# Image chunks in the later passes of a Fourier-layer kernel: one 1 MB load on SyncE and one 1 MB store on GpSimd, in place of two half transfers each on SyncE

## The chip, the cores and the metric

The kernel runs on one core of a Trainium2 chip. The metric is the time of one execution on the device, in microseconds (us). Five engines run their own instruction streams in order: TensorE (PE), VectorE (DVE), ScalarE (ACT), GpSimd (POOL) and SyncE (SP). Any of the last three may issue DMA transfers between the chip's memory (HBM) and the on-chip buffers; here SyncE issues nearly all of them.

## The reference

The input is 64 images of 256 x 256 and 64 text blocks of 77 x 256. A tokenizer of four Fourier layers runs over the images with 32 channels; its result, with the text rows below it, goes through one attention layer and a feed-forward layer that treats half of the rows. Cut to what matters here:

```python
def _fourier_layer(v, W1, W2):            # v: [64 images, 32 channels, 256, 256]
    x_ft = jnp.fft.rfft2(v)
    out1 = jnp.einsum('bixy,ioxy->boxy', x_ft[:, :, :M1, :M2], W1)     # M1 = M2 = 12
    out2 = jnp.einsum('bixy,ioxy->boxy', x_ft[:, :, -M1:, :M2], W2)
    ...
    return jnp.fft.irfft2(out_ft, s=(Sx, Sy))
...
for i in range(L):                        # L = 4
    x1 = _fourier_layer(v, W1, W2)
    x2 = jnp.einsum('bcxy,cd->bdxy', v, w_w[i]) + w_b[i][None, :, None, None]
    v = x1 + x2
    mean = jnp.mean(v, axis=(0, 2, 3), keepdims=True)
    var = jnp.var(v, axis=(0, 2, 3), keepdims=True)
    v = (v - mean) * jax.lax.rsqrt(var + BN_EPS)
    v = v * bn_g[i][None, :, None, None] + bn_b[i][None, :, None, None]
    if i < L - 1:
        v = jax.nn.relu(v)
out = jnp.einsum('bcxy,cu->bxyu', v, q_w) + q_b
```

The normalization is over all 64 images, so every layer has to be complete before its successor can be scaled. The whole of v is 64 x 32 x 256 x 256 numbers of fp32, 537 MB, and is kept in HBM between layers.

## The kernel before, in words

The work is four stages, one after the other. Between them lies `mix` (L428), which multiplies the few kept Fourier coefficients of all images by the layer's weights, writes the result to HBM (`mix_d`) and derives the normalization.

- **Pass 0** (`layer` with i = 0) builds the first v from the coefficients and the image itself and stores it. It loads no v.
- **Passes 1 and 2** (`layer` with i = 1 and 2), the *later passes*, load v of the pass before, compute the new v and store it. `src` and `dst` are two sets of 64 HBM tensors [128, 8, 8, 256] that change roles.
- **The last stage** loads v once more (L980, rows of 8 KB) and does the fourth layer, attention and feed-forward for each image.

An image is cut into eight chunks t = 0 to 7 of 128 partitions x 8 rows x 256 numbers, 1 MB each. In HBM a chunk is 8 KB in a row for each partition. The steps of `layer` for a chunk t of image b are:

- `ld` (L652) loads the chunk into a `vin` tile, in two halves of 512 KB, with rows of 4 KB. The pool `li` has four such tiles in the later passes.
- `pre` (L676) is PE's work: the inverse transform (L682) and the product of the loaded chunk with the layer's weights (L693), both into two pairs of PSUM banks. It then takes a `vo` tile; the pool `lo` has four.
- `evA` and `evB` (L701) evict one bank pair each, with the maximum against zero, into a half of `vo`. The letter `a` or `d` in the order says whether ACT (L705) or DVE (L707) does it.
- `st` (L711) stores `vo` to `dst`, in two halves.
- `turn` (L716) transposes `vo` on DVE (L719) for the next forward transform.
- `prod` (L724) multiplies `vo` with the next layer's weights on PE (L730), and `sqA`/`sqB` (L736) sum its squares on ACT (L741). These give the next variance.

For an image, `am` (L643) has SyncE load the mixed coefficients into one of two `ams` tiles (`load_am`, L621) and POOL scale them (`scale_am`, L628, at L631). `sp` (L662) uses these on PE and `spT` transposes them into the `y_` tiles that `pre` reads. The steps `y` (L752), `half`, `zt`, `x` (L786) and `xo` do the forward transform of the finished image, and `xs` (L803) stores its 72 KB of coefficients.

PSUM is a ring of four slots of two banks, taken by `take` and given back by `close`. `pre` and `prod` take two slots each.

The order of all this is written out by hand. `ORDER[1]` (L137) is one round of the later passes. `@1` marks a step of the next image, `@2` of the one after, `@-1` of the last. Each engine gets its own instructions in just this order. SyncE's share of a round is

```
ld2@1 st4 st5 ld0@1 ld7 ld3@1 st6 ld1@1 st2@1 ld5@1 st0@1 am@2 st7 st1@1 ld4@1 ld6@1 xs@-2 st3@1
```

and POOL's is `am@2` alone. A step that has to wait holds up all that follows it on its engine. PE's `pre` steps come as 5, 6, 2@1, 0@1, 3@1, 7, 1@1, 4@1, so a `vo` tile goes to the fourth chunk after in this list.

Of the kernel before, what the change touches and what calls it, by code (L numbers as in the profile page):

```python
# [153 lines left out]
def tile_fno_fusion_transformer(ctx: ExitStack, tc: tile.TileContext, a, cst_d, grid_d, out):  # L154
    nc = tc.nc
# [390 lines left out]
    def layer(i, st, src, dst, acc):  # L546
# [7 lines left out]
        with ExitStack() as cx:  # L554
# [64 lines left out]
            y_, t32, vin, vo, half_, zts = {}, {}, {}, {}, {}, {}  # L619
# [31 lines left out]

            def ld(b, t, e):  # L652
                vin[b, t] = ip.tile([128, 8, S], F32, name="vin")
                for n in range(2):
                    rows = slice(4 * n, 4 * n + 4)
                    nc.sync.dma_start(vin[b, t][:, rows], src[b][:, t, rows])

            def sp(b, h, e):
                ps = take(("sp", b, h), 1)[0]
# [49 lines left out]
                return run  # L709

            def st_(b, t, e):  # L711
                for n in range(2):
                    rows = slice(4 * n, 4 * n + 4)
                    nc.sync.dma_start(dst[b][:, t, rows], vo[b, t][:, rows])
# [87 lines left out]
            def xs(b, n, e):  # L802
                nc.sync.dma_start(xh_d[i][:, b, :], xos.pop(b).rearrange("p g k -> p (g k)"))  # L803

            run = dict(
                am=am, lx=lx, ld=ld, sp=sp, spT=spT, pre=pre, evA=ev(0), evB=ev(1), st=st_, turn=turn,
                prod=prod, sqA=sq(0), sqB=sq(1), y=y, half=half, zt0=zt(0), zt1=zt(1), x=x_, xo=xo, xs=xs,
            )
# [53 lines left out]
    src = vd[L % 2]  # L862
# [87 lines left out]
    rows = [128, 128, TXT]  # L950
# [283 lines left out]
```

## Time and profile before

| | |
|---|---|
| median of three runs | 11274.17 us (11272.87 to 11285.87) |
| the profiled execution | 11293.58 us, its span 11291.7 us |
| PE, DVE, ACT, POOL busy in the span | 94%, 75%, 57%, 13% |
| HBM read and written | 1733.60 MB and 1696.92 MB |
| v<-vo stores issued by SyncE | 3072 of 512 KB, 1024 in each pass |
| vin<-v loads issued by SyncE | 2048 of 512 KB, 1024 in each later pass |
| PE clock granted, mean | 0.983 |

The profile shows one execution, with times from the start of its span. A group of instructions is named by line, engine, operation and tiles (`v<-vo` writes the HBM tensors v from tile vo). A wait is put down to what came last before the waiting instruction could start. `SPq` is SyncE's instruction stream with its DMA issues; `PEld` is PE's loading of weights, which runs beside its matmuls. Busy shares of PE come from modelled ends of matmuls, so a busy PE is not a PE at its peak. The DMA share is the mean busy share of 16 DMA engines.

### The profile page before, as it was taken

Reading aid. Unit: us, or ns where it says so; the run is one execution under the profiler, and the core shown is the slowest. Engines: PE = TensorE matmul, PEld = TensorE weight load, DVE = VectorE, ACT = ScalarE, POOL = GpSimd, SP = SyncE. Lnnn points to the kernel's source line nnn. Section 1 sums busy time; section 2 is a strip of 40 time slices with the busy share of each in tenths; the row PEclk is TensorE's granted clock in tenths of the full one; section 3 lists DMA queues with packets and bytes.
Section 4 is the critical chain, followed back from the end, with each engine's and each line's share of the span. In section 5 each row is a group of like instructions: output and inputs, shape, how many; then the busy total and the mean of one; then the engine's idle time right before and its main releaser. Section 6 shows DMA issues by size and latency. Waiting matters only on the chain.

```text
span 11291.7 us, 409300 instructions
## 1 busy us (share of the span) xinstructions
PE 10625.0 (94%) x182550; PEld 5738.0 (51%) x182550; DVE 8446.5 (75%) x10381; ACT 6473.1 (57%) x10673; POOL 1442.4 (13%) x2179
## 2 busy tenths in 40 slices
PE   6999999998999999999799999999996999999999
PEld 3555555554444444444444444444443666666666
DVE  6888888887777777777677777777775666666665
ACT  5777777775566655566555566655563333333333
POOL 1111111110000000000000000000000333333333
PEclk8999999998999999999899999999998999999999
DMA  6776676678999999999899999999998555555553
GB/s 213 247 250 244 249 247 248 246 253 320 383 376 382 380 377 372 374 379 379 305 375 380 380 376 378 381 380 376 372 379 291 226 227 228 227 227 228 226 227 140
DMA packets 972544, 3457.29 MB, mean 306 GB/s; under 512 B 149784, under 2 KB 199320, under 8 KB 903832
## 3 DMA queue, kind: packets, MB, share of 16 engines
q1 hardware_dynamic: 905344, 3366.80, 77.8%
q0 software_dynamic: 58288, 60.60, 2.3%
q8 instruction: 1428, 23.40, 0.8%
q10 hardware_dynamic: 7144, 3.72, 0.1%
q14 instruction: 340, 2.79, 0.1%
HBM read 1733.60 MB, written 1696.92 MB: 304 GB/s over the span
## 4 chain that ended last, share of the span: by engine, by line
PE 62%; DMA 20%; DVE 9%; ACT 3%; issue 3%; SPq 2%; POOL 0%; ACTq 0%; DVEq 0%; POOLq 0%
PE ring L752 15%; DMA v<-vo 11%; PE ring L682 9%; PE ring L730 8%; DMA vin<-v 6%; PE ring L693 5%; PE hp L982 4%; PE ring L662 3%; PE pp L1145 3%; PE pp L1156 3%; PE ring L786 2%; DVE vo L707 2%; PE pp L1110 2%; PE pp L1175 2%; PE pp L1072 1%
## 5 line engine op out<-in xcount | busy, mean ns | idle before, releaser
L741 ACT ACTIVATE ring<-ring 128x1024 f32<-128x1024 f32 x3072 | 3115.8, 1014 | 1188.4 <-PE ring L730 1119.5
L719 DVE STREAM_TRANSPOSE t<-vo 128x2048 f32<-128x2048 f32 x1536 | 3465.7, 2286 | 20.9 <-DVE vo L707 0.9
L730 PE MATMUL ring<-vo,w 32*32 32x512 f32 x49152 | 2413.1, 600 | 85.0 <-ACT vo L705 68.3
L707 DVE TENSOR_SCALAR vo<-ring 128x1024 f32<-128x1024 f32 x1280 | 1544.5, 1221 | 1199.7 <-PE ring L693 806.6
L705 ACT ACTIVATE vo<-ring 128x1024 f32<-128x1024 f32 x1792 | 1791.7, 1023 | 1044.1 <-PE ring L693 500.9
L752 PE MATMUL ring<-t,cst 32*32 32x512 f32 x49152 | 2072.0, 599 | 51.0 <-issue 44.9
L752 PEld LDWEIGHTS ring<-t,cst 32*32 32x32 f32 x49152 | 913.4, 103 | 925.6 <-issue 622.6
L730 PEld LDWEIGHTS ring<-vo,w 32*32 32x32 f32 x49152 | 803.2, 103 | 1070.2 <-issue 407.1
L693 PE MATMUL ring<-vin,ws 32*32 32x512 f32 x32768 | 1287.8, 603 | 22.9 <-issue 16.2
L682 PE MATMUL ring<-cst,y 24*128 24x256 f32 x16384 | 1230.3, 402 | 77.0 <-DVE vo L707 61.7
L682 PEld LDWEIGHTS ring<-cst,y 24*128 24x128 f32 x16384 | 789.5, 185 | 993.2 <-DVE vo L707 392.4
L631 POOL TENSOR_TENSOR ams<-ams,bns 48x512 f32<-48x512 f32 x384 | 400.5, 1043 | 6989.4 <-DMA ams<-mix 6510.1
L670 DVE STREAM_TRANSPOSE y<-ring 128x1024 f32<-128x1024 f32 x384 | 763.1, 1987 | 329.5 <-PE ring L662 328.5
L682 PE MATMUL ring<-mv,y 29*128 29x256 f32 x8192 | 705.3, 403 | 36.3 <-ACT ring L741 19.6
L682 PEld LDWEIGHTS ring<-mv,y 29*128 29x128 f32 x8192 | 456.9, 185 | 369.0 <-ACT ring L741 209.3
L786 PEld LDWEIGHTS ring<-cst,zt 128*128 128x128 f32 x4608 | 533.6, 193 | 177.1 <-ACT vo L705 114.2
L762 ACT COPY half<-ring 128x1024 f32<-128x1024 f32 x192 | 194.4, 1013 | 731.4 <-PE ring L752 731.4
L1183 POOL DMA_DIRECT2D out_dram<-o x1024 | 508.2, 505 | 659.0 <-DVE o L1178 616.9
L741 ACT ACTIVATION_READ_ACCUMULATOR ring<-ring 128x1 f32 x3072 | 585.6, 191 | 0.0
L786 PE MATMUL ring<-cst,zt 128*128 128x96 f32 x4608 | 565.6, 280 | 6.1 <-DVE zt L770 5.7
L770 DVE STREAM_TRANSPOSE zt<-ring 128x1024 f32<-128x1024 f32 x192 | 377.4, 1965 | 248.1 <-PE ring L752 248.1
L662 PE MATMUL ring<-ams,cst 49*128 49x512 f32 (+1 forms) x1536 | 450.6, 642 | 99.1 <-POOL ams L631 37.2
(374 smaller groups left out, 9762.6 us busy)
## 6 DMA issues: line engine op xcount, KB each, us to landing
v<-vo SPq DMA_DIRECT2D x3072, 512.0 KB, 7.8
vin<-v SPq DMA_DIRECT2D x2048, 512.0 KB, 9.1
ch<-v SPq DMA_DIRECT2D x512, 1024.0 KB, 12.5
mix<-ob SPq DMA_DIRECT2D x96, 512.0 KB, 5.6
ams<-mix SPq DMA_DIRECT2D x384, 96.0 KB, 8.0
xin<-in_x_dram SPq DMA_DIRECT2D x16, 1024.0 KB, 6.5
mv<-in_x_dram POOLq DMA_DIRECT2D x256, 64.0 KB, 7.4
out_dram<-o POOLq DMA_DIRECT2D x1024, 16.0 KB, 3.0
```

Of the source, the lines that this page charges most:

```text
L662: nc.tensor.matmul(ps[:, n, :], lhsT=EX[hv, 128 * h:128 * h + 128], rhs=ams[b % 2][hv], start=True, stop=True, skip_group_check=True,)
L670: nc.vector.transpose(y_[b, h].rearrange("p q c -> p c q"), ring[key][0][1].rearrange("p n (c k) -> p (n c) k", k=32),)
L682: nc.tensor.matmul(ps[n][:, 256 * r:256 * r + 256], lhsT=y_[b, t // 4][32 * n:32 * n + K, q:q + 4, :].rearrange("p q c -> p (q c)"), rhs=m ...
L693: nc.tensor.matmul(ps[n][32 * j:32 * j + 32], lhsT=ws[32 * n:32 * n + 32], rhs=v[32 * n:32 * n + 32, 2 * j:2 * j + 2, :], start=False, sto ...
L705: nc.scalar.activation(to, ring[key][h][1], AF.Relu)
L707: nc.vector.tensor_scalar(to, ring[key][h][1], 0.0, None, ALU.max)
L719: nc.vector.transpose(t32[b, t // 2][:, :, 8 * (t % 2):8 * (t % 2) + 8, :].rearrange("p y s c -> p s y c"), vo[b, t].rearrange("p s (y l) ...
L730: nc.tensor.matmul(ps[n][32 * j:32 * j + 32], lhsT=w4[i + 1][32 * n:32 * n + 32], rhs=vo[b, t][32 * n:32 * n + 32, 2 * j:2 * j + 2, :], st ...
L741: nc.scalar.activation(ps, ps, AF.Square, accum_out=acc[:, at:at + 1])
L752: nc.tensor.matmul(ps[n][32 * j:32 * j + 32], lhsT=FYT[32 * n:32 * n + 32, k, :], rhs=t32[b, j][32 * n:32 * n + 32, k].rearrange("p s c -> ...
L786: nc.tensor.matmul(ps[:, 0, 96 * g:96 * g + 96], lhsT=zt_[:, h, k0:k0 + 4, :].rearrange("p k c -> p (k c)"), rhs=FX[:, h, 48 * r:48 * r + ...
L1183: nc.gpsimd.dma_start(out[b, 64 * n + 16 * g:64 * n + 16 * g + 16].rearrange("(p t) d -> p t d", t=2), o[32 * g + 8 * n:32 * g + 8 * n + 8 ...
```

## The change

In `ld` the two half loads become one load of the whole chunk, still issued by SyncE. In `st` the later passes issue one store of the whole chunk from GpSimd's queue; pass 0 keeps its two half stores on SyncE. The order, the pools and all other steps are as they were. SyncE's share of a round of the later passes is then the `ld` steps, the loads of `am` and `xs`; POOL's is `st4 st5 st6 st2@1 st0@1 am@2 st7 st1@1 st3@1`.

```diff
             def ld(b, t, e):
                 vin[b, t] = ip.tile([128, 8, S], F32, name="vin")
-                for n in range(2):
-                    rows = slice(4 * n, 4 * n + 4)
-                    nc.sync.dma_start(vin[b, t][:, rows], src[b][:, t, rows])
+                nc.sync.dma_start(vin[b, t], src[b][:, t])
...
             def st_(b, t, e):
+                if i:
+                    nc.gpsimd.dma_start(dst[b][:, t], vo[b, t])
+                    return
                 for n in range(2):
                     rows = slice(4 * n, 4 * n + 4)
                     nc.sync.dma_start(dst[b][:, t, rows], vo[b, t][:, rows])
```

## The prediction, made before the changed kernel had run

> **What bounds the kernel now.** I read the page's slices first, because the change touches only two of the four stages. One core runs the work; the bandwidth row shows where.
>
> ```profile
> DMA  6776676678999999999899999999998555555553
> GB/s 213 247 250 244 249 247 248 246 253 320 383 376 382 380 377 372 374 379 379 305 375 380 380 376 378 381 380 376 372 379 291 226 227 228 227 227 228 226 227 140
> ```
>
> A slice is 282 us. Slices 10 to 19 and 20 to 30, near 377 GB/s, are the two later passes (i=1, 2), which load and store every chunk; the first pass only stores, the last stage only loads. Next the engines in one of these passes, from the windows view (columns: window, its length, busy time of PE, PE's weight loads, DVE, ACT, POOL, clock, DMA share, GB/s).
>
> ```profile
> 2700.00:5400.00 2700.00, 2588.29 (x55106) 1224.46 (x55105) 2021.65 (x1128) 1625.06 (x2559) 123.24 (x118) 1.00 0.98 377
> ```
>
> PE and DMA both look full; neither quite is. An image takes 45.3 us (SyncE's ams loads start at 3626.7, 3671.5, 3717.3, 3762.4, 3808.2, 3853.2). PE's steps, at the closest spacing that the timeline shows (32 small matmuls in 1.07 us, 16 of L682 in 1.08, the 24 of L786 in 2.84, L662 in 1.06), add to about 8x1.07x3 + 8x1.08 + 2.84 + 2.1 = 39 us. An image moves 16.8 MB of chunks and 0.27 MB of the rest. In 1 us slices of one image the DMA runs flat at about 415 GB/s for some 25 us and swings between 25 and 430 in the other 20, with a mean near 330; 17.05 MB at 415 would be 41 us. So both have about a tenth to spare, and dependencies between them make up the 45.3 us. The chain of waits of that window gives DMA v<-vo 20.1% and DMA vin<-v 11.7% of it. Who waited says what this costs (engine, line, releaser: total us, times, longest):
>
> ```profile
> ACT vo L705 <- DMA v<-vo: 125.6, 94, 3.1
> DVE vo L707 <- DMA v<-vo: 124.4, 95, 3.0
> PEld ring L662 <- POOL ams L631: 37.4, 33, 1.3
> PEld ring L693 <- DMA vin<-v: 12.0, 24, 1.0
> ```
>
> The evictions of a new chunk wait until the store of the chunk that held the same vo buffer (four of them) has landed; the two engines wait side by side, so it is one loss of about 125 us in 2700. Why stores land late shows in the view of L714, in the later pass and then in the first:
>
> ```profile
> DMA to landing us min/median/max: 2.8/8.9/12.7
> DMA to landing us min/median/max: 2.6/4.9/10.0
> ```
>
> The same 512 KB takes 8.9 us instead of 4.9, since it stands behind loads in one queue. It is also issued late: SyncE's own waits in that pass are
>
> ```profile
> SPq L714 <- ACT vo L705: 495.3, 127, 8.2
> SPq L714 <- DMA v<-vo: 312.0, 347, 2.3
> SPq L714 <- DMA vin<-v: 240.8, 273, 2.4
> ```
>
> that is, it stands at a store until ACT has evicted, with loads behind it, and then is held back by its full DMA queue, one issue each 1.5 us.
>
> **What the Trainium skill says.** "DMA: Bandwidth & Descriptors", section "Issuing engines are not separate DMA queues": transfers of all issuers run on the same 16 DMA engines and interleave, so another issuer brings no bandwidth. I count none; no run shown here puts two large streams on two queues. The same page, "Queues, rings and completion order": each DMA engine takes turns between the queue rows that hold work, a packet at a time. A store on its own row then passes the loads' backlog. The trace shows the one-queue side of it only (8.9 against 4.9 us). "SBUF — State Buffer", section "SBUF: two separate sides": GpSimd cannot write its descriptors while VectorE holds both ports in a two-port mode. "VectorE: DVE Perf Modes", "Why PSUM operands drop a tier": fp32 from PSUM runs at the base rate. The trace agrees: L707 reads PSUM, 1024 elements in 1221 ns, and the transpose L719 2048 in 2286 ns, both over 1 ns an element. I expect no such lock.
>
> **The change, part by part.** An image now costs SyncE 16 half loads, 16 half stores, two ams loads and one xh store; after it, 8+2+1. There are 128 images in the two passes.
>
> *Halves to wholes.* 4 KB rows become 8 KB rows. In the last stage 1 MB loads with 8 KB rows (ch<-v) run near 419 GB/s when the queue is full (9030 to 9045 us), against 415 with 4 KB rows: 1%. DMA volume is not what ends the image, so I cost this at nothing; if it were, 1% of 41 us is 0.4 us an image, 52 us. Against it, a whole chunk lands as one, so the first half's eviction can wait up to 0.5 MB/415 GB/s = 1.3 us longer where it waits at all. That is 1.6 places an image (95 in 59.6), 265 us at worst; the earlier issue of the store covers it.
>
> *Stores to GpSimd.* 8 issues an image. The nearest rows are POOL's loads of mv (L638) and xh (L845), 563 and 552 ns each, the latter for 4 MB: 4.5 us on an engine with 2.1 us of work in 45.3, hidden. A lower bound is zero, since POOL is off the path. The descriptors cost latency too: 64 KB loads from GpSimd take 7.4 us to land in pass one beside 4.9 us for 96 KB from SyncE, so I add 2.5 us. Half of 415 GB/s moves 1 MB in 5.1 us, with 2.5 us more 7.6; alone at full rate 5.0. Before: 8.9 from issue, and issued 2 to 13 us after the evictions (st6: evictions end near 3611.7, issue 3614.0; st3 of the next image: 3626.7 and 3639.6). The tightest reuse I find is chunk 2 to chunk 1 of an image, 3618.4 to 3630.7, 12.3 us: 7.6 fits.
>
> *Loads alone on SyncE.* They go when vin is free: chunk 4 at about 3627 instead of 3635.3, chunk 0 at 3607.2 instead of 3609.2. Little is gained directly, since PE waits for vin 12.0 us in the pass, most of it the 0.33 us that a weight load idles anyway. ams is asked for at about 3621 instead of 3626.7.
>
> *Sum.* Windows 2700 to 5400 and 5700 to 8400 hold 119 of the 128 images (factor 1.074). Store waits: DVE 124.4+133.6 = 258, times 1.074 = **277 us**. What passes to PE is a choice: in the image read, chunk 3's evictions wait 1.03 us and PE's next step, prod, shows a 0.77 us gap, but other waits fall where PE has work or waits for a PSUM pair anyway. I take half, **139**. ams: 37.4+33.3 = 71 us of weight-load idle in 63 waits, 1.1 each, where 0.9 is usual before that step: 0.25 us x 63 x 1.074 = **17**. vin: 25.3 us, 0.33 of each usual: **10**. Together 166, of an upper bound of 277+76+27 = 380. The profiled execution took 11293.6 us (span 11291.7), 19.4 above the median of 11274.2. 11293.6 - 166 = 11127.6, or **11108** on the median's scale. After the store waits, what is late next is the eviction-to-PSUM-ring step (DVE vo <- PE ring L693 and the weight loads held by DVE vo).
>
> **Rivals.**
>
> *All of it passes through.* The chain's 32% of DMA speaks for it; PE's 39 us and DMA's 41 leave room. 380 us: 10894. Chance 0.13.
>
> *Nothing passes through.* In the first pass stores hardly stall (DVE 5.1 us, ACT 24.3 in 1800), yet an image takes 36.4 us where the same PE count gives 30.6: nearly 6 us of gaps from evictions and PSUM alone, as many as here. Then a freed store only lets another wait surface: 0 to 30 us gained, 11244 to 11274. Against: DVE is busy 89% there and 75% here. Chance 0.13.
>
> *Slower: stores behind the ams wait on GpSimd.* POOL runs in order. Its list is now st4, st5, st6, st2, st0, am (wait for the ams load, then two scalings, 2.2 us), st7, st1, st3. Today ams takes 10 us to land and POOL waits for it in nearly every image. Asked for at 3621 it lands at 3631, is scaled by 3633, and three stores leave by 3634.5; 3 MB at half rate is 15.2 us, plus 2.5: 3652. Chunk 3's buffer is wanted by chunk 5's evictions at 3652.5. It just fits; if ams lands later than 11 us after its issue, or if the loads get more than half the DMA, every us is lost. With ams as late as today the store is 5 us late; half passed on is 2.5 x 128 = 320, less the 166: 11430. For it: a margin under 1 us. Against: loads end before that, so stores get more than half, and ams stands behind fewer loads. Chance 0.17.
>
> *The change does not do what it says*, 8 KB rows being cut to 4 KB packets: in the last stage 59,296 packets are of 8 KB or more, about 464 loads x 128 rows, so rows travel whole. It would cost nothing in any case.
>
> **How the numbers follow.** Forecast 0.57, all 0.13, nothing 0.13, slower 0.17. Within 0.2%, 22 us (about what a measurement of this kernel can tell from no change), lies some 0.08 of the third case; its rest gains just over that. Faster 0.75, same 0.08, slower 0.17. The range reaches down to 10960, which leaves out the farthest part of the full gain (some 0.06), and up to 11340, which takes in the milder half of the slower case.
>
> **What would show it.** Right: the waits of ACT and DVE on v<-vo fall below a third, the image falls to 44 us (GB/s of the slices up to 388), SyncE no longer waits for ACT, POOL shows 1024 issues near 0.55 us, DMA leaves the chain. Wrong: evictions wait as much as before with stores landing over 12 us; POOL's st7 starts only after ams and evictions wait right after; or the store waits vanish and PE's gaps behind DVE and ACT grow by as much.

## The result and the profile after

The changed kernel takes **11313.56 us** (median, 11308.88 to 11326.04), the kernel before in the same runs 11274.56 (11265.47 to 11291.58). The ratio is 1.0034, 95% interval [1.0025, 1.0043]: 39 us slower, where 166 faster had been forecast. The profiled execution took 11314.35 us, 20.8 more than that of before; the two profiles thus show about half of the difference in the medians.

What the change was aimed at did move. The waits of the middle of pass 1 (2700 to 5400 us; total us, times, longest), then the chain of the whole span by engine, before and after:

```profile
DVE vo L705 <- PE ring L691: 353.0, 284, 4.2
PEld ring L753 <- issue: 257.0, 487, 2.9
DVE vo L705 <- DMA v<-vo: 107.8, 73, 3.9
ACT vo L703 <- DMA v<-vo: 71.9, 74, 3.2
PEld ring L691 <- DMA vin<-v: 1.3, 4, 0.3
```

```profile
PE 62%; DMA 20%; DVE 9%; ACT 3%; issue 3%; SPq 2%; POOL 0%; ACTq 0%; DVEq 0%; POOLq 0%
PE 73%; DVE 10%; DMA 9%; issue 4%; ACT 3%; SPq 0%; POOL 0%; ACTq 0%; DVEq 0%; POOLq 0%
```

With pass 2's window (ACT 61.0, DVE 36.8; before 131.8 and 133.6), the waits of evictions for stores fell from 257 us to 133 on ACT and from 258 to 145 on DVE: to half, not to nothing. PE's waits for vin are nearly gone, those for POOL's ams wholly. DMA fell from 20% to 9% of the chain and PE rose from 62% to 73%. Yet the window holds no more work (length, then busy time of PE, weight loads, DVE, ACT, POOL, clock, DMA share, GB/s):

```profile
2700.00:5400.00 2700.00, 2581.68 (x54896) 1220.74 (x54888) 2021.36 (x1126) 1621.09 (x2548) 374.41 (x592) 1.00 0.95 376
```

That is 54,896 matmuls in place of 55,106. Two landing views bear on why only half of the waits went: stores of L711, then loads of L654.

```profile
DMA to landing us min/median/max: 5.7/11.1/15.9
DMA to landing us min/median/max: 4.9/11.3/14.3
```

A 1 MB store lands 11.1 us after its issue; the forecast had 7.6. Its working took a single store with half of the bandwidth, but stores overlap. In this window the 114 of 474 that had no other store under way when they were issued landed in 8.3 us (median), those with one or two in 11.0 and 12.0. POOL's timeline shows three in a row after the scaling of ams:

```profile
3638.52 2.16 POOL L631 TENSOR_TENSOR ams<-ams,bns 48x512 f32<-48x512 f32 x2 [9.62 <-PE ring L660]
3640.63 1.64 POOL L711 DMA_DIRECT2D v<-vo  x3
```

They landed at 3648.7, 3651.2 and 3653.6.

**Where the gain went.** From the starts of PE's instructions in the trace I cut each round of the later passes in three (means over 103 rounds): the *store part*, from `pre` of chunk 3 to the first `sp`, where most late stores are waited for; the *y section*, from that `sp` to `pre` of chunk 4 (both `sp`, eight `y`, one `prod`); and the rest.

| us a round | store part | y section | rest | round |
|---|---|---|---|---|
| before | 10.43 | 13.48 | 21.53 | 45.44 |
| after | 9.74 | 14.23 | 21.67 | 45.64 |
| difference | -0.70 | +0.75 | +0.14 | +0.20 |

The store part gives back 0.70 us and the y section takes 0.75. The standard error of a mean is 0.05 us for the store part and 0.06 to 0.11 for the others. The net 0.20 x 128 is 25 us, near the 21 between the profiled executions. What PE lacks in the y section shows in the page's groups: L752 before and L753 after, the same matmuls and their weight loads (busy, mean ns | idle before, what ended most of it):

```profile
L752 PE MATMUL ring<-t,cst 32*32 32x512 f32 x49152 | 2072.0, 599 | 51.0 <-issue 44.9
L752 PEld LDWEIGHTS ring<-t,cst 32*32 32x32 f32 x49152 | 913.4, 103 | 925.6 <-issue 622.6
```

```profile
L753 PE MATMUL ring<-t,cst 32*32 32x512 f32 x49152 | 2116.8, 600 | 82.0 <-issue 75.4
L753 PEld LDWEIGHTS ring<-t,cst 32*32 32x32 f32 x49152 | 914.9, 103 | 998.5 <-issue 691.8
```

One matmul takes as long as before. What grew is "issue", time in which PE waited for nothing that the profile shows: 31 us before the matmuls, 69 before the weight loads. One line of the page's list of queues, which the prediction did not use, names a suspect (packets, MB, share of 16 engines):

```profile
q8 instruction: 1429, 23.41, 0.8%
```

PE runs 182,550 matmuls and as many weight loads. Spread over these 365,100 instructions, 23.41 MB is 64 bytes for each, and a packet of 16.4 KB is 256 of them. I take it from this count that the queue carries PE's own program, 7.2 packets in a round; if one comes late, PE stands still. The gaps fit: compared with the median gap at the same place of the round, PE loses over 500 ns 1.37 times a round before (1.40 us) and 1.98 times after (2.08 us). I call these gaps *stalls*. Some 63% of them, before, and 65%, after, end 1.25 to 1.5 us after the end of such a packet, where 5% of places picked at random lie. They also come back every 255.7 of PE's records, so they shift by a fixed step from round to round, as blocks of 256 instructions do.

The y section has most of the growth: its stalls went from 0.60 to 1.20 us a round, 0.60 of the 0.75 that it lost. Of those 58 stalls before and 118 after (112 rounds each), 57 and 108 end 1.2 to 1.6 us after a packet. PE's waits for the other engines did not grow there: its weight loads wait 1.7 us a round behind ACT, DVE and POOL before and 1.0 after. So in the kernel after, most of what the y section lost is PE without instructions.

### The profile page after: what moved, and what is told of

Same layout as the page of the kernel before. It is cut to its first block, busy times and chain, and to the rows that moved or that the text cites. A ratio compares the mean times of both kernels' runs of the same rounds, so it can differ in the third digit from the quotient of the medians.

```text
span 11312.5 us, 405471 instructions
## 1 busy us (share of the span) xinstructions
PE 10623.1 (94%) x182550; PEld 5739.4 (51%) x182550; DVE 8455.8 (75%) x10381; ACT 6479.4 (57%) x10673; POOL 1985.2 (18%) x3203
## 3 DMA queue, kind: packets, MB, share of 16 engines
q8 instruction: 1429, 23.41, 0.8%
## 4 chain that ended last, share of the span: by engine, by line
PE 73%; DVE 10%; DMA 9%; issue 4%; ACT 3%; SPq 0%; POOL 0%; ACTq 0%; DVEq 0%; POOLq 0%
PE ring L753 17%; PE ring L680 12%; PE ring L731 11%; PE ring L691 8%; DMA v<-vo 7%; PE hp L983 4%; DVE vo L705 4%; PE ring L787 3%; PE ring L660 3%; PE pp L1146 3%; PE pp L1157 3%; PE pp L1111 2%; PE pp L1176 2%; PE pp L1073 1%; DVE t L720 1%
## 5 line engine op out<-in xcount | busy, mean ns | idle before, releaser
L731 PE MATMUL ring<-vo,w 32*32 32x512 f32 x49152 | 2448.5, 600 | 53.1 <-ACT vo L703 32.6
L753 PE MATMUL ring<-t,cst 32*32 32x512 f32 x49152 | 2116.8, 600 | 82.0 <-issue 75.4
L753 PEld LDWEIGHTS ring<-t,cst 32*32 32x32 f32 x49152 | 914.9, 103 | 998.5 <-issue 691.8
L691 PE MATMUL ring<-vin,ws 32*32 32x512 f32 x32768 | 1241.6, 604 | 15.5 <-issue 15.0
L711 POOL DMA_DIRECT2D v<-vo x1024 | 549.9, 539 | 3727.7 <-DVE vo L705 2566.2
L787 PEld LDWEIGHTS ring<-cst,zt 128*128 128x128 f32 x4608 | 533.2, 193 | 175.3 <-ACT vo L703 110.5
L787 PE MATMUL ring<-cst,zt 128*128 128x96 f32 x4608 | 565.2, 279 | 7.4 <-DVE zt L771 7.2
```

Source lines behind the costliest of these rows:

```text
L691: nc.tensor.matmul(ps[n][32 * j:32 * j + 32], lhsT=ws[32 * n:32 * n + 32], rhs=v[32 * n:32 * n + 32, 2 * j:2 * j + 2, :], start=False, sto ...
L711: nc.gpsimd.dma_start(dst[b][:, t], vo[b, t])
L731: nc.tensor.matmul(ps[n][32 * j:32 * j + 32], lhsT=w4[i + 1][32 * n:32 * n + 32], rhs=vo[b, t][32 * n:32 * n + 32, 2 * j:2 * j + 2, :], st ...
L753: nc.tensor.matmul(ps[n][32 * j:32 * j + 32], lhsT=FYT[32 * n:32 * n + 32, k, :], rhs=t32[b, j][32 * n:32 * n + 32, k].rearrange("p s c -> ...
L787: nc.tensor.matmul(ps[:, 0, 96 * g:96 * g + 96], lhsT=zt_[:, h, k0:k0 + 4, :].rearrange("p k c -> p (k c)"), rhs=FX[:, h, 48 * r:48 * r + ...
```

## The experiments

Theory **F** (fetch): the transfers delay PE's instruction packets, most with two queues of 8 KB rows together, and PE stalls where its instructions are densest. Against it: **P**, stores held back behind the ams wait in GpSimd's order (the slower rival of the prediction); **G**, given back: evictions freed of stores wait for PSUM instead, so that no store wait is worth anything. Ratios are to the kernel before on the same chip.

**Whole chunks, one queue (e1).** To the kernel after:

```diff
-                    nc.gpsimd.dma_start(dst[b][:, t], vo[b, t])
+                    nc.sync.dma_start(dst[b][:, t], vo[b, t])
```

> Whole chunks both ways, but the stores stay on SyncE: the row size alone is changed, not the issuer. Three theories stand. Instructions: in the changed kernel PE's irregular stalls (over 500 ns beyond the usual gap at the same place of the round, most of them ending 1.25 to 1.5 us after an instruction packet has arrived) grew from 1.4 to 2.1 us a round, because two data queues of 8 KB packets stand before the instruction fetch; that ate what the freed stores gave. Given back: PE's gaps come from evictions and PSUM, and a store that lands earlier is worth nothing. POOL order: the stores behind the ams wait cost the time. Instructions theory: if the second queue does it, stalls stay at 1.4 us and the time is 11250 to 11280; if the 8 KB packets do it, stalls near 2 us and 11310 to 11360. Given back: 11275 within 15. POOL order: 11275 within 15, since GpSimd has no stores here.

11291.43 us, 1.001 [1.0001, 1.0018]. Round 45.40, y section 13.67.

**Halves, two queues (e2).** To the kernel before:

```diff
-                    nc.sync.dma_start(dst[b][:, t, rows], vo[b, t][:, rows])
+                    (nc.gpsimd if i else nc.sync).dma_start(dst[b][:, t, rows], vo[b, t][:, rows])
```

> Stores of the later passes on GpSimd, but all transfers stay halves with 4 KB rows: the issuer alone is changed. Instructions theory: if the second queue does it, stalls of 2 us a round and about 11310; if the packet size does it, stalls of 1.4 us, store waits halved and about 11200. Given back: 11275 within 15. POOL order: about 11310, as in the changed kernel, since the ams wait stands in GpSimd's list as there.

11277.11 us, 0.9996 [0.9988, 1.0005]. Store part 9.74 as in the kernel after, y section 13.70. So the second queue alone brings the gain of the store part. Most of it is given back: the y section takes 0.2 us of it and the rest of the round 0.24, where DVE now waits for stores 0.96 us a round (0.05 before). The time ends at nothing that can be measured. Neither the rows alone nor the queue alone lengthens the y section by more than about 0.2 us.

**After, with 4 KB rows (e5).** The HBM tensors become [128, 2, 8, 4, 256], so that a whole chunk has two rows of 4 KB a partition.

```diff
-    vd = [dram.tile([128, 8, 8, S], F32, name=f"v{b}_{n}") for n in range(2) for b in range(B)]
+    vd = [dram.tile([128, 2, 8, 4, S], F32, name=f"v{b}_{n}") for n in range(2) for b in range(B)]
...
-                    nc.gpsimd.dma_start(dst[b][:, t], vo[b, t])
+                    nc.gpsimd.dma_start(dst[b][:, :, t], vo[b, t].rearrange("p (h r) y -> p h r y", h=2))
```

> The changed kernel (one whole transfer of 1 MB each way, two queues), but v lies in HBM as two half chunks, so that every row is of 4 KB. So far: irregular PE stalls of over 500 ns are 1.4 us a round before, 1.6 and 1.3 with one queue of 8 KB rows, 1.4 and 1.5 with two queues of 4 KB rows, 2.0 and 2.1 with two queues of 8 KB rows. Instructions theory: an instruction packet waits for one packet of each data queue, so with 4 KB packets the stalls fall to 1.5 us and the time to that of the two queues of halves, 11260 to 11285. Whole-landing theory (a buffer that is released and filled as a whole is what costs, not the packet): stalls stay at 2 us or the time stays at 11313 within 10. Given back: 11275 to 11313, says little.

11349.78 us, 1.0064 [1.0051, 1.0077], and read by stage: y section 13.67, round 45.45, as in the kernel before. Nearly the whole loss is in the last stage, whose loads now have 4 KB rows as well: from the last matmul of the passes (L786, here L787) to the end of the span it takes 2778 us in place of 2717. With e1 and e2 this closes the square: only two queues **and** 8 KB rows together give the long y section.

It also shows that a short y section is not enough. The store part takes 9.66 us, 0.77 less than before, and yet the round is no shorter: the rest of the round grew by 0.56 us, with 1.75 us a round of DVE's waits for stores (0.05 before) and 0.83 us of stalls (0.53 before). Stalls come to 1.69 us a round in all, between before and after and over the 1.5 that F had. In e2 and in e5 the gain of the store part is thus lost without the long y section, in the rest of the round.

**The ams load issued early (e3):** in the kernel after (a step `al` right after `ld2@1`; `am` only scales).

```diff
-    ... "ld2@1 st4 evB5.d ..."
+    ... "ld2@1 al@2 st4 evB5.d ..."
```

> The changed kernel with SyncE asking for ams some 20 us earlier in the round (right after the first load), so that GpSimd finds it landed and the stores of chunks 7, 1 and 3 leave as soon as they are evicted. POOL order: the 39 us that were lost come back and more, 11270 or below. Instructions: no change, 11313 within 15, or a little better as the burst of three stores in the y section is spread. Given back: no change, 11313 within 15.

11322.75 us, 1.0032 [1.002, 1.0045]. POOL no longer waits for ams, and evictions wait for stores only about a seventh less (107.8 and 71.9 us in the kernel after):

```profile
DVE vo L710 <- DMA v<-vo: 92.5, 61, 3.5
ACT vo L708 <- DMA v<-vo: 60.1, 62, 2.9
```

P falls: with that wait gone, nothing of the 39 us comes back. The y section stays long (14.24).

**A fifth vo tile in the kernel before (e4)**, paid with a vin tile.

```diff
-            ip = pool("li", 2 if i == 0 else 4, reuse_waits="tile")
+            ip = pool("li", 2 if i == 0 else 3, reuse_waits="tile")
...
-                for n, k in (("lo", 4), ...)
+                for n, k in (("lo", 5 if i else 4), ...)
```

> The kernel before with five vo tiles in place of four and three vin tiles in place of four (the memory holds no more): a store has one more chunk's time to land, with one data queue and 4 KB rows. Instructions theory: store waits of ACT and DVE fall from 125 us in 2700 to under 30, instruction stalls stay at 1.4 us a round, and about 1 us a round passes to PE: 11150 to 11200, unless three vin tiles starve PE. Given back: store waits fall as well, and the time stays at 11275 within 15. POOL order: says nothing here.

11455.53 us, 1.0156 [1.0142, 1.017]. Store waits fell to 17.9 us of ACT and 7.0 of DVE, but PE now starved for loads (the weight loads' line):

```profile
PEld ring L693 <- DMA vin<-v: 110.1, 130, 2.2
```

So it says nothing on the worth of a store wait. The next bounds it.

**The kernel before, with a quarter of each load (e7).**

```diff
-                    rows = slice(4 * n, 4 * n + 4)
+                    rows = slice(n, n + 1)
...
-                                rhs=v[32 * n:32 * n + 32, 2 * j:2 * j + 2, :], start=False, stop=True,
+                                rhs=v[32 * n:32 * n + 32, 0:2, :], start=False, stop=True,
```

> The kernel before with three quarters of the load left out: of a chunk's eight rows two are loaded (in two transfers), and PE uses these in place of all eight, so all of PE's work stays and the result is another. DMA carries 10.8 MB a round in place of 17.05. Instructions theory: irregular stalls fall from 1.4 us a round to below 0.4 (in the first pass, at a DMA share of 0.70, they are 0.2), the store waits end too, and a round falls from 45.4 to 43 to 43.8, 11000 to 11110 in all. Given back: PE's gaps are set by evictions and PSUM, a round stays above 45.0 and the time above 11230 even with the DMA engines free.

10929.2 us, 0.9692 [0.9678, 0.9705]. Its window:

```profile
2700.00:5100.00 2400.00, 2343.71 (x52217) 1167.91 (x52215) 1922.69 (x1069) 1543.48 (x2425) 116.95 (x112) 1.00 0.71 256
```

With the DMA at 0.71 of its time the round is 42.63 us: store part 9.33, y section 12.64, rest 20.66. G falls: all three parts shorten, with the same PSUM and evictions. The store part can win 1.1 us a round, 141 us in all; the y section holds another 0.84 and the rest 0.87. The stalls are all but gone (0.08 us a round). The run takes the waits for stores and for vin and the stalls away at once, so it does not say what one of them is worth while the DMA stays full.

**The same in the kernel after (e8)**, with the same `rhs`.

```diff
-                nc.sync.dma_start(vin[b, t], src[b][:, t])
+                nc.sync.dma_start(vin[b, t][:, 0:2], src[b][:, t, 0:2])
```

> The changed kernel with the same three quarters of the load left out (one transfer of two rows each chunk), stores whole on GpSimd. Instructions theory: as the kernel before with a quarter of the loads, 11000 to 11110, stalls below 0.4 us a round; the two kernels then differ by less than 15 us. If GpSimd's queue itself is what costs (its order, its latency), this one stays 20 to 40 us behind the other. Given back: above 11230 as the other.

10971.53 us, 0.9726 [0.9711, 0.9741], 42 us behind its partner. F's 15 us missed; the 20 to 40 us written down for a cost of GpSimd's queue itself came nearer. Nearly all of the round's 0.24 us is again in the y section (12.87 against 12.64). Stalls there are 0.19 us a round against 0.08, so they explain about half of it. Whatever else whole stores on GpSimd do to that section needs no full DMA (its share is 0.68 here) and stays open; the loads, too, differ between the two, one transfer of 2 KB rows a chunk against two of 1 KB rows.

**Each part of the change alone.** First the loads, with stores as before (e9):

```diff
-                for n in range(2):
-                    rows = slice(4 * n, 4 * n + 4)
-                    nc.sync.dma_start(vin[b, t][:, rows], src[b][:, t, rows])
+                nc.sync.dma_start(vin[b, t], src[b][:, t])
```

> The first half of the change alone: whole loads of 8 KB rows, stores still two halves on SyncE. So far the y section of a round (from the first step sp to the next pre) takes 13.5 us before, 13.7 with one queue of 8 KB rows, 13.6 with two queues of 4 KB rows, 14.2 with two queues of 8 KB rows, 12.6 with a quarter of the loads. Instructions theory: one queue, so the y section stays at 13.5 to 13.7, store waits stay near 125 us in 2700, and the time is 11270 to 11290. If whole loads were what costs, it would be 11300 or more.

11281.87 us, 1.0001 [0.9993, 1.0009]. Then the stores, with half loads as before (e10):

```diff
+                if i:
+                    nc.gpsimd.dma_start(dst[b][:, t], vo[b, t])
+                    return
```

> The second half of the change alone: whole stores of 8 KB rows on GpSimd, loads still two halves of 4 KB rows. Instructions theory: one packet of 8 KB and one of 4 KB stand before an instruction packet, so the y section lies between, 13.8 to 14.0, store waits fall by a third to a half, and the time is 11275 to 11300. If GpSimd's issue itself costs, it is 11313 as in the whole change.

11573.08 us, 1.0259 [1.0245, 1.0273]. This missed. The store waits went as good as entirely, but the loads fell behind:

```profile
PEld ring L693 <- DMA vin<-v: 131.7, 88, 3.5
PE ring L693 <- DMA vin<-v: 64.9, 57, 2.6
```

The loads' landing view has its longest at 17.7 us, against 12.1 before:

```profile
DMA to landing us min/median/max: 3.3/10.7/17.7
```

Loads of 4 KB rows beside stores of 8 KB rows get too little of the DMA (e12, below, measures the shares); the two parts of the change belong together.

**Transfers cut by partitions (e6).** In the kernel after, each chunk moved as two halves of 64 partitions, rows still 8 KB. The loads (the stores likewise):

```diff
-                nc.sync.dma_start(vin[b, t], src[b][:, t])
+                for n in range(2):
+                    hv = slice(64 * n, 64 * n + 64)
+                    nc.sync.dma_start(vin[b, t][hv], src[b][hv, t])
```

> The counterpart: two transfers of 512 KB for each chunk and way, on the two queues, but halved by partitions, so that rows are of 8 KB. Instructions theory: stalls of 2 us a round as in the changed kernel, 11300 to 11325. Whole-landing or number-of-transfers theory: as the two queues of halves, stalls of 1.5 us, 11260 to 11285.

12056.81 us, 1.0692 [1.0677, 1.0707]. The DMA carried 335 GB/s at a share of 0.99; a load's 8 KB packet took 428 ns on average, against 341 in the kernel after. PE's stalls rose to 6.5 us a round, as F has it in direction; the size was not foreseen, and why such packets take longer stays open.

**The fetch by itself (e11).** PE runs 96 steps shaped like `y` (1536 small matmuls) ten times, beside streams of loads and stores that it does not use.

```
for r in range(1, 97):
    for m in range(4):
        for n in range(4): nc.tensor.matmul(ps[n][32 * j:32 * j + 32], ...)   # 32x32 by 512
```

> No part of the reference is computed. PE runs ten stretches of 96 steps of 32 small matmuls like those of y, whose data never change and wait for nothing, beside 32 loads and 32 stores of 1 MB: none; one queue of halves; one queue of wholes; two queues of halves; two queues of wholes; none; and the last four again in the opposite order. Instructions theory: without DMA a stretch takes 96 x 0.88 = 85 us; with one queue or with 4 KB rows it takes 3 to 10 percent more, with two queues of 8 KB rows the most, at least 3 percent above two queues of 4 KB rows. If the DMA traffic does not reach PE, all ten take the same within 1 percent. If only the amount of traffic counts, the four kinds take the same and only the two stretches without are shorter.

Without transfers 99.3 and 99.6 us a stretch; with one queue of halves 143.3 and 143.8, one of wholes 145.3 and 144.2, two of halves 145.8 and 146.1, two of wholes 151.9 and 148.8. The base of 85 us and the few per cent both missed: with nothing to wait for but its instructions, a stretch of PE takes 44 to 53% longer. Idle before L193, the only matmul:

```profile
L193 PE MATMUL ps<-t,w 32*32 32x512 f32 x30720 | 1084.8, 616 | 453.9 <-issue 289.2
```

It has some 25 stalls of about 2 us a stretch, one for each 16 KB packet (239 packets in all for 61,440 instructions) and ending 1.4 to 1.5 us after one (medians of the stretches), and two without transfers. That the traffic starves PE of instructions is shown. Two queues of wholes come last, as F says, but PE's clock was below full for part of these stretches, for longest in them, so the order of the kinds is not proven. A second set of rows (e12):

> As the kernel with PE's stream alone, with other rows: no DMA's place is the first; then one queue of 2 KB rows, two queues of 2 KB rows, two queues with loads of 4 KB and stores of 8 KB, the other way round, two queues of 8 KB; and the middle four in the opposite order. Theory that DMA engines take turns by packets: with 4 KB loads against 8 KB stores the store queue moves twice the bytes of the load queue, near 275 and 137 GB/s, and the reverse the other way round; that would be why whole stores with half loads left PE waiting for vin. Rival, turns by bytes or by transfers: both queues move about 205 GB/s each. Instructions theory: a stretch takes 143 to 145 us with one queue of 2 KB rows, at most 146 with two of 2 KB, 147 to 149 with mixed rows, and again 149 to 152 with two of 8 KB.

All kinds lie between 135.7 and 147.2 us, two queues of 8 KB here 144.2: the stand-alone stream does not tell the kinds apart. It could hardly do so, because in e12 transfers of one kind still run during the next stretch (4 KB stores, for instance, until 870 us in the stretch from 810 that was meant for 8 KB in both). The shares have to be read where one kind is alone. From 505 to 605 us these are 4 KB loads (q1) beside 8 KB stores (q0), from 675 to 760 8 KB loads beside 4 KB stores (packets, MB, share of 16 engines):

```profile
q0 software_dynamic: 3813, 27.73, 66.3%
q1 hardware_dynamic: 3843, 14.00, 34.5%
```

```profile
q1 hardware_dynamic: 3199, 23.31, 65.3%
q0 software_dynamic: 3357, 12.21, 35.4%
```

Both queues move about as many packets, and the one with 8 KB rows twice the bytes: 140 GB/s of loads beside 277 of stores, then 274 beside 144. With 8 KB in both (970 to 1010 us) it is 210 and 210. These are the shares of strict turns by packet, as the theory had them, and not those of the rival. They also fit e10: there, too, loads of 4 KB rows stand beside stores of 8 KB.

**A pair with few instructions in y.** In the later passes each `y` step issues 2 matmuls of 128x128 instead of 16 of 32x32, in the kernel before (e13) and in the kernel after (e14).

```diff
+                if i:
+                    for m in range(2):
+                        g = 2 * (k % 2) + m
+                        nc.tensor.matmul(
+                            ps[g], lhsT=ID, rhs=t32[b, g][:, k].rearrange("p s c -> p (s c)"),
+                            start=k < 2, stop=k > 5, skip_group_check=True,
+                        )
+                    return
```

> The kernel before, but in the later passes each step y issues 2 matmuls of 128x128 by 512 columns in place of 16 of 32x32 by 512; two of the sp kind take 1.06 us on PE, the 16 small ones 1.07, so PE's time stays and its instructions in the eight y steps fall from 512 records to 64. The values of y are not the Fourier sums any more; what is evicted, stored and waited for stays. Instruction theory: some of the stalls of 500 ns and more (1.4 us a round before) lie in the y section and go; the round falls by 0.3 to 1.0 us, time 11150 to 11240. Rival (the y section's time is set by VectorE, PSUM or the bursts of stores): within 20 us of before.

11706.19 us, 1.0381 [1.0366, 1.0397]. The size missed: a dense step takes 1.82 us of PE (802.6 us of busy time for 442 steps) and not 1.07, so the pair runs on a longer round, 48.67 us, with the DMA at 0.91.

> The kernel after, with the same replacement in y. Instruction theory: the 0.69 us a round that the y section lost by the change vanish, 0.2 at most is left, while the 0.66 us that evictions gain stay: the kernel after becomes faster than e13 by 0.3 to 0.6 us a round, 40 to 80 us. Rival (VectorE, PSUM or the bursts of stores lengthen that section): the section stays 0.5 us or more longer than in e13, and the kernel ends 20 to 45 us slower than e13, as after does against before. A result between, equal within 20 us, would say that both have a part.

11636.1 us (11627.61 to 11646.73, against 11703.38 to 11708.68), 1.0323 [1.0305, 1.034] to the kernel before: **70 us faster than its partner**, inside the 40 to 80 that F gave.

| us a round | store part | y section | rest | round | stalls over 500 ns |
|---|---|---|---|---|---|
| before, dense y | 10.42 | 17.51 | 20.74 | 48.67 | 0.28 |
| after, dense y | 9.79 | 17.52 | 20.87 | 48.19 | 0.25 |
| difference | -0.62 | +0.01 | +0.13 | -0.48 | -0.03 |

The gain of the store part is the same as in the real pair, the rest too, and the loss in the y section is gone. The weight loads of the y step in the second of them (total us, times, longest):

```profile
PEld ring L753 <- issue: 467.3, 1578, 0.8
```

The pauses are short and regular, 0.8 us at the longest, where the kernel after had 2.9. This fits F, but it does not decide by itself. The longer round leaves the DMA a little room (shares of 0.91 and 0.89, against 0.98 and 0.95 in the real pair), and the pair does not say how much comes from the fewer instructions and how much from that room. The y section is 4 us longer and the same in every round (standard error under 0.001 us), so PE alone sets it, and a longer wait of another engine could hide there. That no such wait ate the gain in the real pair rests on its traces, where the stalls grew and PE's waits for other engines did not.

## Why the prediction was wrong

- **What bounds the kernel.** Right that dependencies between PE and DMA make up the round, and that evictions waiting for stores are one of them. Wrong in what the rest was: PE's floor was counted as matmuls at their closest spacing, 39 us, and the gaps between as dependencies. Up to 1.4 us a round of them were PE without instructions. With three quarters of the loads gone e7 is some 350 us faster, but that is these stalls and the waits for loads and stores together, so it is no measure of the rival "all of it passes through".
- **Store landing, 7.6 us.** Mis-sized: 11.1. It priced one store with half the bandwidth, and a store alone did take 8.3; but three of four had others beside them. The slower rival's own working had three stores in a burst, 15.2 us, and the forecast should have used it. So the waits fell to half and not below a third.
- **Half of the waits passes to PE.** Not the failing term. In the store part DVE's waits for stores fell from 2.16 to 0.51 us a round and PE got 0.70 back, four tenths, not far from the half. What the forecast missed is that waits come up anew elsewhere: in the rest of the round DVE waits 0.75 us for stores, 0.05 before. Measured product 0.70 x 128 = 89 us, forecast 139.
- **ams 17 and vin 10.** The waits are gone as forecast; what they gave by themselves was not separated. (71 us in 63 waits are 1.12 each, 0.22 over the usual 0.9, so the first term should have been 15.)
- **"I cost this at nothing" (halves to wholes, and no bandwidth from another issuer).** This is the step that failed: the sum has no term for what the change costs PE. Each half holds by itself: whole loads (e9) 1.0001, the second queue (e2) 0.9996. Together they cost 0.75 us a round in the y section, 95 us, as large as the gain, and 0.60 of the 0.75 are stalls that follow PE's instruction packets. I asked only what the rows and the queue do to the transfers, and not who else is a customer of the same DMA engines. The page had named one: q8 instruction. This term alone does not make up the 166 us, though. Without the long y section e2 and e5 gained nothing either: there, waits for stores and stalls came up in the rest of the round instead. Whether any order of stores keeps the gain while the DMA is this full (a share of 0.95 to 0.99 in these runs) is not shown; in e14, at 0.89, it was kept.
- **What the Trainium skill says.** "DMA: Bandwidth & Descriptors", section "Issuing engines are not separate DMA queues", held: 376 GB/s after, 377 before. Section "Queues, rings and completion order" has each DMA engine take turns between rows that hold work, a packet at a time; I drew the store's benefit from it and not the cost to a third row with a 16 KB packet that PE waits for. The shares in e12 agree with it: equal numbers of packets, twice the bytes for rows of 8 KB. The lock of GpSimd was rightly not expected: an issue took 531 to 597 ns.
- **The rivals.** None had this mechanism. P fell to e3. G fell to e7 as far as evictions and PSUM are meant to set the round; e2 and e5 do give their gain back, but to stores and stalls. Of the signs listed, the nearest was "the store waits vanish and PE's gaps behind DVE and ACT grow by as much": the gaps grew, but behind PE's own issue.
- **Smaller points.** POOL's 1024 issues of 539 ns cost nothing visible, as forecast; SyncE's loads no longer wait for ACT; the first pass stayed (2348.3 us from its first `pre` to its last L786 or L787, before and after) and the last stage too, within some 5 us (2722 and 2717).

**Open.** Why two queues with 8 KB rows delay the instruction packets at the start of the y section more than either alone. Counted from a fixed place in each block of 256 instructions (a mark of mine; only differences count), the next packet starts 0.2 us later after the change than before (standard errors 0.04), and 0.5 to 0.7 us later in the tenth of the round where the y section begins. With two queues of 4 KB rows (e2, e5) the mean delay is the same as after the change; only in that tenth are they 0.5 us better. The stand-alone stream did not tell why. What adds half of the y section's loss in e8 is open as well. Nor do the profiles show all of the 39 us between the medians: the profiled pair is 21 apart, and the other 18 lie within the spread of single runs (11265 to 11292 before).

## What to carry to other kernels

Where the DMA is nearly full and PE runs on thousands of small matmuls, count PE's own instruction stream as a DMA customer and look for growing "issue" time before weight loads, not only for waits on tiles. A wait that a change removes is worth only what the next contention leaves of it, so price bursts of transfers as bursts and ask for each freed transfer whom it now runs beside. Look, too, where a freed wait comes up again: in e2 and e5 the same waits for stores returned later in the round. Row size and issuing queue, which did nothing singly in e1 and e2, may cost together, and loads and stores on different queues want rows of like size, since they took turns by packet in e12.

## What the runs showed of the hardware that I had not expected

- A stream of 32x32 matmuls that waits for no data slows from 99 to between 136 and 152 us beside streams of loads and stores that fill the DMA (e11, e12): one stall of about 2 us for each 16 KB of instructions.
- 1 MB moved as two transfers of 64 partitions each is far worse than as one: 335 GB/s and 428 ns for an 8 KB packet, and 6.9% of the kernel's time (e6).
- Whole 1 MB transfers of 4 KB rows cost the last stage, which only loads, 61 us in 2717, 2.2% (e5).
- A 128x128 fp32 matmul of 512 columns took 0.91 us in the stream of e13 (half of 1.82), where two such with 49 rows, in `sp`, take 1.13 together there (124.2 us of busy time for 110 steps).
